# How fc's weight columns reach the partitions: matrix products on TensorE, or row transfers and a block transpose on VectorE

## The chip, the cores and the metric

The kernel runs on one core of one Trainium2 chip. A core has a matrix engine (TensorE, in the profile PE, with its weight loads as PEld), a vector engine (VectorE, DVE), a scalar engine (ScalarE, ACT), GpSimd (POOL), a queue engine for transfers (SyncE, SP) and 16 DMA engines that all of them share. The metric is the device time of one execution in microseconds, as the median of several runs.

## The reference

Three layers of a "compressed interaction network" and one linear read-out, on a batch of 1024 rows (F = 39 fields, E = 64 numbers per field, H = 64 outputs per layer):

```python
def _cin_layer(Xk, X0, W, b):
    Wr = W.reshape(O, Hk, Fdim)
    return jnp.einsum('bhe,bfe,ohf->boe', Xk, X0, Wr) + b[None, :, None]
X0 = sparse_embedding
Xk = X0
outs = []
for W, b in ((W0, b0), (W1, b1), (W2, b2)):
    Xk = _cin_layer(Xk, X0, W, b)
    outs.append(Xk.sum(axis=-1))
cin_output = jnp.concatenate(outs, axis=-1)
return cin_output @ fc_w.T + fc_b
```

`fc_w` is one row of 192 numbers: 64 for each layer. Since only sums over E of the layers' outputs reach the result, a part of the read-out can be drawn into the weights: layer 2 and fc's third part become a small matrix V2, and V2 with W1 and fc's second part becomes weights that are multiplied with products of two fields.

## The kernel before

**The main loop.** The batch is cut into 32 blocks of 32 rows, each 2048 columns (row times E). Of every block the products of pairs of fields are formed by VectorE, 128 pairs at a time (line 219 for six full tiles of pairs, line 221 for a rest that two blocks share), and multiplied by TensorE with prepared weights `wa` into four PSUM banks (line 561; the rest by lines 581 and 592). Four product buffers let VectorE run ahead. ScalarE and VectorE finish a block (lines 609, 611, 622). The operands `r`, `u` and `v` of the products are rows of x, gathered by GpSimd with indirect transfers (line 174) whose row numbers stand in the tile `lists`. The order of the work on each engine is written out by hand; nothing is reordered.

**The head.** Before the first product of line 561 the weights must be made, and the first rows gathered. In the order of TensorE:

- `spin` (line 279) multiplies constants into a bank that nobody reads: a dummy, which only keeps the engine occupied. Lines 287, 341, 411, 509, 513 and 669 call it.
- fc's columns. `fc_w` is loaded as one row on one partition (line 250, SP's queue). GpSimd writes its second and third part with each number doubled (`double`, line 320, four copies), and TensorE turns rows into columns, as products with a single 1 (`turn`, line 323): two for the doubled columns behind the first dummy, three more (columns for the finishing of blocks and for the read-out) at lines 510 to 512. They land in the bank `small`.
- V2: `fc2`, which VectorE makes from the first doubled column and a mask (line 357), times `w2s` (line 403, eight instructions), then two block transposes of VectorE (line 422), then two small products that spread the result (line 435), and VectorE writes `v2` (lines 448 and 455; the last one uses the second doubled column).
- The transposes of W0 (line 415), and T: `v2` times `w1s` (line 484, eight instructions), whose four results VectorE transposes (line 493). From there come the pair weights (lines 500 to 528), the turned weights (lines 545 to 547) and the first real product.

**VectorE in the head** runs, in its order: memsets (lines 245 to 249), a chain of small operations on 128 numbers for the index lists (lines 309 and 343 to 363, the lists are ready with lines 362 and 363), in the midst of it `fc2` (line 357), then `unit` and `twice` (lines 371 to 375), more of the index work (lines 380 to 384), and the transposes of line 422.

**The transfers in the head.** ScalarE's queue issues `w2s`, the first half of x's first block (`xh`), `w0s`, `w1s` and the second half, in this order (lines 252 to 260). GpSimd writes a row of ones to DRAM (line 366) and then gathers; its first gather (line 389) needs the first `xh` and the lists.

```python
def turn(dst, row):
    nc.tensor.matmul(dst, row, one, start=True, stop=True)
```

Of the kernel before, what the change touches and what calls it, by code (L numbers as in the profile page):

```python
# [54 lines left out]
F32 = mybir.dt.float32  # L55
I32 = mybir.dt.int32
AF = mybir.ActivationFunctionType
ALU = mybir.AluOpType
AX = mybir.AxisListType

B, F, E, H = 1024, 39, 64, 64
# [14 lines left out]
MM = 512  # L76
# [10 lines left out]
NY = 3  # L87
# [60 lines left out]
def cin_kernel(ctx: ExitStack, tc: tile.TileContext, x, w0t, b0, w1, b1, w2, b2, fc_w, fc_b, out):  # L148
    nc = tc.nc
# [3 lines left out]
    const = ctx.enter_context(tc.tile_pool(name="const", bufs=1))  # L153
# [9 lines left out]
    def bank(name):  # L163
        return psum.tile([128, MM], F32, name=name, tag="po")
# [23 lines left out]
    wa = const.tile([128, NCHUNK, 3 * H], F32, name="wa")  # L188
    columns = const.tile([128, 3], F32, name="columns")
    v2 = const.tile([128, 128], F32, name="v2")  # L190
    v2v = v2.rearrange("p (low s b) -> p low s b", s=2, b=32)
    twice = const.tile([128, H, 2], F32, name="twice")
    b2s = const.tile([H, 1], F32, name="b2s")
    b1s = const.tile([128, 1], F32, name="b1s")
    b0s = const.tile([128, 1], F32, name="b0s")
    fc0s = columns[:, 1:2]
    fcb = const.tile([NY * 32, 1], F32, name="fcb")
# [8 lines left out]
    ones = const.tile([16, 2, 128], F32, name="ones")  # L206
# [18 lines left out]
    with prep as prep:  # L225
# [3 lines left out]
        flat = prep.tile([128, 4, NA, 32], F32, name="flat")  # L229
        fcrow = prep.tile([1, 3 * H], F32, name="fcrow")  # L230
        fcrow2 = prep.tile([1, 2, H, 2], F32, name="fcrow2")
        fc2 = prep.tile([128, H], F32, name="fc2")
# [10 lines left out]


        nc.vector.memset(ones, 1.0)
        nc.vector.memset(fc2, 0.0)
        nc.vector.memset(v2, 0.0)
        nc.vector.memset(warm, 0.0)
        nc.vector.memset(wfin[0:H], 1.0)
        nc.sync.dma_start(fcrow, fc_w)  # L250
        def load_half(k):
# [21 lines left out]
        pw = [bank("pw") for _ in range(2)]  # L273
        small = bank("small")


        def spin(n=1, cols=MM // 2):
            for _ in range(n):
                nc.tensor.matmul(  # L279
                    idle[:, 0:cols],  # L280
                    nc.const_aps.tensor(1.0, (128, 128), F32),
                    nc.const_aps.tensor(1.0, (128, cols), F32),
                    start=True,
                    stop=True,
                )
# [13 lines left out]
        def step(x, at, by, out=None):  # L299

            out = new() if out is None else out
            nc.vector.tensor_scalar(out, x, at, by, ALU.is_ge, ALU.mult)
            return out
# [8 lines left out]
        for i in range(NT):  # L312
            at = OFFSET[i] - 3 * K + (0 if i < NT - 1 else -F)
            for k, by in enumerate((STEP[i], BASE[i], at)):
                nc.gpsimd.memset(shifts[:, k, i : i + 1], float(by))
        one = ones[0:1, 0, 0:1]

        def double(dst, src):
            for s in range(2):
                nc.gpsimd.tensor_copy(dst[:, :, s], src)  # L320

        def turn(dst, row):
            nc.tensor.matmul(dst, row, one, start=True, stop=True)

        def turn_row(h, at, row, k):
            turn(small[h : h + H, at : at + 1], row[:, k * H : k * H + H])

        def turn_twice(at, row, k):
            turn(small[:, at : at + 1], row[:, k].rearrange("p h s -> p (h s)"))

        double(fcrow2[:, 1], fcrow[:, 2 * H : 3 * H])
        double(fcrow2[:, 0], fcrow[:, H : 2 * H])
        for k, series in enumerate((U_STEPS, V_STEPS)):
# [4 lines left out]
        nc.gpsimd.memset(bothv[0:H, :, F], 0.0)  # L338
        for at, k in ((0, 1), (6, 0)):
            turn_twice(at, fcrow2, k)  # L340
        spin(1, 3 * MM // 4)

        nc.vector.tensor_copy(row, place)
        step(row, F, 1.0, j)
        step(row, K + ONLY, 1.0, late)
# [10 lines left out]
        )  # L356
        nc.vector.tensor_scalar(fc2[:, 0::32], mask, small[:, 0:1], None, ALU.mult)
        step(wide[:, 1], F, -float(F), wide[:, 2])
# [95 lines left out]

        nc.vector.tensor_scalar(v2v[:, 0, :, F - 32], mask, small[:, 6:7], None, ALU.mult)

# [39 lines left out]
        for k, a in groups:  # L496
# [4 lines left out]
            if k > 1:  # L501
# [6 lines left out]
                )  # L508
        spin(1, MM)
        for h in (0, H):  # L510
            turn_row(h, 1, fcrow, 0)
        turn_row(0, 2, fcrow, 2)
        spin(1, MM)
        first = [prods.tile([128, BLK], F32, name="p", tag="p") for _ in range(3)]
# [125 lines left out]
    def last_weights(pk):  # L640
        for low, at, n in ((1, 0, 32), (0, 32, F - 32)):
            nc.tensor.matmul(
                pk[at : at + n, 0:1], v2v[:, low, 0, 0:n], b1s, start=True, stop=True
            )
        fc1 = v2v[:, 0, 0, F - 32 : FT - 32]
        total = pk[0 : NY * 32, 1:2]
        nc.tensor.matmul(total, b1s.to_broadcast([128, NY * 32]), fc1, start=True, stop=False)
        nc.tensor.matmul(
            total, b2s.to_broadcast([H, NY * 32]), columns[0:H, 2:3], start=False, stop=True
        )  # L650
        nc.scalar.copy(wfin[H : H + F], pk[0:F, 0:1])
        nc.scalar.activation(kfin, total, AF.Identity, bias=fcb, scale=float(E))
# [10 lines left out]
    for k, (n, c) in enumerate(steps[:3]):  # L663
# [11 lines left out]
        else:  # L675
            product(n, c, halves[0], p[n, c])
    nc.scalar.copy(columns[0:H, 1:3], small[0:H, 1:3])
    nc.scalar.copy(fc0s[H:128], small[H:128, 1:2])
    for n, c in steps[:3]:
# [128 lines left out]
```

## Time and profile before

| | |
|---|---|
| median of 3 runs | 733.39 us (732.57 to 735.92) |
| the profiled execution's own time | 733.53 us |
| its span, first to last instruction | 731.5 us |
| mean granted TensorE clock | 0.999 |
| PE busy | 726.7 us, 99% of the span |
| DVE busy | 638.2 us, 87% |
| POOL busy | 401.0 us, 55% |
| DMA | mean 270 GB/s |
| first product of line 561 begins | 17.40 us after the span's start |

All times inside the profile are counted from the first instruction; 2.0 us of the device time lie around the span. [...] an interval of "busy" TensorE can also be slow TensorE: the time from one product to the next has to be read beside it. [...]

### The profile page before, as it was taken

To read this page: it belongs to the slowest core of one execution; us is meant where nothing else is said; L and a number is where in the kernel's file an instruction comes from. 1 tells how busy PE (TensorE), PEld (TensorE's weight loads), DVE (VectorE), ACT (ScalarE), POOL (GpSimd) and SP (SyncE) were. 2 spreads that over 40 slices of the span, in tenths; PEclk is the share of its full clock that TensorE was granted. 3 is DMA by queue.
4 is the path that set the end of the run, shared out by engine and by line. 5 is a ranking of instruction groups with operands and counts; after the bars stand their busy time and mean duration, and the time that the engine had idled before them with its cause. 6 is when DMAs were issued, how large, how long until landed. Compare 5 with 4: busy or idle time off the path is not lost.

```text
span 731.5 us, 6359 instructions
## 1 busy us (share of the span) xinstructions
PE 726.7 (99%) x2379; PEld 315.3 (43%) x2379; DVE 638.2 (87%) x521; ACT 167.0 (23%) x240; POOL 401.0 (55%) x254
## 2 busy tenths in 40 slices
PE   9999999999999999999999999999999999999998
PEld 4444444444444444444444444444444444444443
DVE  6989699988889988889988889888898988889885
ACT  3332121222212222121222212222121221212222
POOL 6779869636555445754537555455654547545300
PEclk9999999999999999999999999999999999999999
DMA  8986796989575787757679575886767777566700
GB/s 273 378 322 251 304 367 247 382 324 366 219 283 222 284 339 279 277 226 280 273 288 326 230 280 222 310 345 233 280 244 278 299 287 280 197 267 234 288 0 1
DMA packets 65983, 197.24 MB, mean 270 GB/s; under 512 B 40110, under 2 KB 40179, under 8 KB 45984
## 3 DMA queue, kind: packets, MB, share of 16 engines
q0 software_dynamic: 28784, 185.56, 64.9%
q1 hardware_dynamic: 35468, 9.29, 5.5%
q10 hardware_dynamic: 1700, 1.99, 0.9%
q8 instruction: 18, 0.29, 0.2%
q14 instruction: 13, 0.11, 0.0%
HBM read 196.76 MB, written 10.60 MB: 283 GB/s over the span
## 4 chain that ended last, share of the span: by engine, by line
PE 87%; DVE 5%; issue 3%; DMA 2%; POOL 2%; ACT 0%; DVEq 0%; POOLq 0%
PE po L561 80%; PE po L581 4%; DVE p L219 3%; PE po L592 2%; POOL r L174 2%; DVE g L611 1%; DMA r<-xd,lists 1%; DMA b0s<-in_b 1%; PE idle L279 1%; DVE sums L622 1%; DVE pairs L528 0%; PE pv L403 0%; PE pt L484 0%; PE pw L415 0%; PE pv L484 0%
## 5 line engine op out<-in xcount | busy, mean ns | idle before, releaser
L561 PE MATMUL po<-p,wa 128*128 128x512 f32 x1536 | 665.2, 593 | 0.6 <-DVE p L219 0.5
L219 DVE TENSOR_TENSOR p<-r 128x2048 f32<-128x2048 f32 (+2 forms) x198 | 433.8, 2223 | 72.8 <-PE po L561 63.8
L174 POOL DMA_INDIRECT r<-xd,lists x156 | 316.3, 2028 | 264.4 <-issue 255.0
L561 PEld LDWEIGHTS po<-p,wa 128*128 128x128 f32 x1536 | 289.7, 190 | 371.9 <-issue 353.7
L609 ACT ACTIVATE z<-po,columns 64x512 f32<-64x512 f32 x128 | 87.4, 683 | 374.2 <-PE po L592 216.0
L611 DVE SCALAR_TENSOR_TENSOR g<-po,b0s,z 64x512 f32<-64x512 f32 x128 | 95.9, 749 | 9.3 <-ACT z L609 5.3
L604 ACT COPY g<-r 39x1024 f32<-39x1024 f32 x64 | 66.7, 1043 | 161.5 <-DVE sums L622 129.7
L622 DVE TENSOR_REDUCE sums<-g 103x16 f32<-103x1024 f32 x62 | 75.6, 1219 | 2.1
L174 POOL DMA_INDIRECT u<-xd,lists x16 | 40.1, 2509 | 7.1 <-issue 4.6
L581 PE MATMUL po<-p,wa 32*64 32x512 f32 x512 | 31.6, 600 | 0.0
L174 POOL DMA_INDIRECT v<-xd,lists x16 | 26.5, 1659 | 4.9 <-issue 4.9
L221 DVE TENSOR_TENSOR p<-u,v 128x1024 f32<-128x1024 f32 x16 | 19.5, 1216 | 0.0
L581 PEld LDWEIGHTS po<-p,wa 32*64 32x64 f32 x512 | 9.4, 131 | 20.1 <-issue 20.1
L592 PE MATMUL po<-u,wa 32*64 32x512 f32 x256 | 17.0, 587 | 0.0
L174 POOL DMA_INDIRECT r<-xh,lists x8 | 8.0, 1002 | 4.7 <-DVE tmp L384 2.6
L592 PEld LDWEIGHTS po<-u,wa 32*64 32x64 f32 x256 | 5.8, 132 | 8.1 <-issue 8.0
L279 PE MATMUL idle<-const-float32-1.0 128*128 128x512 f32 (+2 forms) x12 | 7.7, 732 | 0.8 <-PEq L795 0.8
L528 DVE TENSOR_TENSOR pairs<-both 128x2 f32<-128x2 f32 (+27 forms) x59 | 6.1, 172 | 0.3
L546 ACT COPY wa<-tr 128x128 f32<-128x128 f32 x8 | 2.1, 266 | 15.3 <-PE tr L545 15.3
L279 PEld LDWEIGHTS idle<-const-float32-1.0 128*128 128x128 f32 x12 | 2.5, 253 | 1.9 <-issue 1.7
L168 POOL DMA_DIRECT2D xd<-in_x x3 | 3.2, 1056 | 0.0
L461 ACT COPY both<-pw 64x468 f32<-64x468 f32 (+2 forms) x4 | 1.9, 472 | 4.4 <-issue 4.3
(97 smaller groups left out, 55.2 us busy)
## 6 DMA issues: line engine op xcount, KB each, us to landing
xd<-in_x SPq DMA_DIRECT2D x28, 312.0 KB
r<-xd,lists POOLq DMA_INDIRECT x156, 9.1
xd<-in_x POOLq DMA_DIRECT2D x3, 312.0 KB
w2s<-in_w ACTq DMA_DIRECT2D x1, 624.0 KB
w1s<-in_w ACTq DMA_DIRECT2D x1, 624.0 KB
w0s<-in_w0t ACTq DMA_DIRECT2D x1, 380.2 KB
xh<-in_x ACTq DMA_DIRECT2D x2, 156.0 KB
xd<-xh SPq DMA_DIRECT2D x2, 156.0 KB
```

The costliest lines, as they stand in the source:

```text
L174: nc.gpsimd.indirect_dma_start(dst, None, table, bass.IndirectOffsetOnAxis(ap=lists[:, k : k + 1], axis=0))
L219: nc.vector.tensor_tensor(p[:, cols], r[:, i, cols], r[:, k, cols], ALU.mult)
L221: nc.vector.tensor_tensor(p[:, 0:SUB], ut[n // 2 % 2], vt[n // 2 % 2], ALU.mult)
L279: nc.tensor.matmul(idle[:, 0:cols], nc.const_aps.tensor(1.0, (128, 128), F32), nc.const_aps.tensor(1.0, (128, cols), F32), start=True, sto ...
L528: nc.vector.tensor_tensor(out, diagonal(a, b, sa, sb), diagonal(b, a, sb, sa), ALU.add)
L561: nc.tensor.matmul(po[n][m], wa[:, c, side : side + 2 * H], p[:, bass.ts(m, MM)], start=n % 2 == 0 and c == 0, stop=n % 2 == 1 and c == NP ...
L581: nc.tensor.matmul(dst[half * H : half * H + H], wa[rows, NPAIR, at : at + H], p[rows, bass.ts(side, MM)], start=t >= 2, stop=t < 2 and ha ...
L592: nc.tensor.matmul(dst[half : half + H], wa[rows, NPAIR + 1, H : 2 * H], ut[n // 2 % 2][rows, bass.ts(side, MM)], start=False, stop=t < 2,)
L604: nc.scalar.copy(gt[H : H + F], rt[n % 2][0:F, 0, bass.ts(m, SUB)])
L609: nc.scalar.activation(z[one], po[n][m][other], AF.Identity, bias=fc0s[other])
L611: return lambda: nc.vector.scalar_tensor_tensor(g[n][m // 2][0:H, at], po[n][m][one], b0s[one], z[one], ALU.add, ALU.mult)
L622: nc.vector.tensor_reduce(sums[:, b_at : b_at + SB], g[n][m // 2].rearrange("p (b e) -> p b e", e=E), AX.X, ALU.add,)
```

## The change

fc's columns no longer go through GpSimd and TensorE. Three small row transfers on SP's queue bring pieces of `fc_w` to four partitions (0, 32, 64 and 96): one brings fc's second and third part, 16 numbers to a partition, for the doubled columns, and two bring its first and third part, 32 numbers to a partition. VectorE clears both tiles first, copies the 16 numbers twice each into the row tile, and transposes it in blocks of 32 by 32 (one instruction, 128x128); each column of interest is then the first column of a block in `columns`, in SBUF. The copy and the transpose stand in VectorE's order behind `row <- place` and ahead of the index chain.

On TensorE the five `turn` products (ten instructions) are gone, the second dummy has 512 columns in place of 384, and the two dummies behind T stand together. GpSimd's four copies, the bank `small` and ScalarE's two copies out of it are gone. Everything else is as before; its lines have other numbers.

```diff
-    columns = const.tile([128, 3], F32, name="columns")
+    columns = const.tile([128, 4, 32], F32, name="columns")
-    fc0s = columns[:, 1:2]
+    fc1t, fc2t, fc0s, fc2s = (columns[:, k, 0:1] for k in range(4))
...
-        fcrow = prep.tile([1, 3 * H], F32, name="fcrow")
-        fcrow2 = prep.tile([1, 2, H, 2], F32, name="fcrow2")
+        fcq = prep.tile([128, 2, 16], F32, name="fcq")
+        fcrow = prep.tile([128, 4, 32], F32, name="fcrow")
...
+        nc.vector.memset(fcq, 0.0)
+        nc.vector.memset(fcrow, 0.0)
         nc.vector.memset(ones, 1.0)
...
-        nc.sync.dma_start(fcrow, fc_w)
+        nc.sync.dma_start(
+            fcq[0::32], fc_w.rearrange("o (k g j) -> (o g) k j", k=3, j=16)[:, 1:3]
+        )
+        halves_of = fc_w.rearrange("o (k g j) -> (o g) k j", k=3, j=32)
+        for h in (0, H):
+            nc.sync.dma_start(fcrow[h : h + H : 32, 2:4], halves_of[:, 0:3:2])
...
-        double(fcrow2[:, 1], fcrow[:, 2 * H : 3 * H])
-        double(fcrow2[:, 0], fcrow[:, H : 2 * H])
...
-        for at, k in ((0, 1), (6, 0)):
-            turn_twice(at, fcrow2, k)
-        spin(1, 3 * MM // 4)
+        spin(1, MM)
 
         nc.vector.tensor_copy(row, place)
+        nc.vector.tensor_copy(
+            fcrow[:, 0:2].rearrange("p k (j s) -> p k j s", s=2),
+            fcq.unsqueeze(3).to_broadcast([128, 2, 16, 2]),
+        )
+        nc.vector.transpose(
+            columns.rearrange("p k j -> p (k j)"), fcrow.rearrange("p k j -> p (k j)")
+        )
         step(row, F, 1.0, j)
...
-        nc.vector.tensor_scalar(fc2[:, 0::32], mask, small[:, 0:1], None, ALU.mult)
+        nc.vector.tensor_scalar(fc2[:, 0::32], mask, fc2t, None, ALU.mult)
...
-        nc.vector.tensor_scalar(v2v[:, 0, :, F - 32], mask, small[:, 6:7], None, ALU.mult)
+        nc.vector.tensor_scalar(v2v[:, 0, :, F - 32], mask, fc1t, None, ALU.mult)
...
-        spin(1, MM)
-        for h in (0, H):
-            turn_row(h, 1, fcrow, 0)
-        turn_row(0, 2, fcrow, 2)
-        spin(1, MM)
+        spin(2, MM)
...
-            total, b2s.to_broadcast([H, NY * 32]), columns[0:H, 2:3], start=False, stop=True
+            total, b2s.to_broadcast([H, NY * 32]), fc2s[0:H], start=False, stop=True
...
-    nc.scalar.copy(columns[0:H, 1:3], small[0:H, 1:3])
-    nc.scalar.copy(fc0s[H:128], small[H:128, 1:2])
```

More of the change, by code (lines that the diff above doesn't have):

```diff
@@ L273, in cin_kernel @@
         pw = [bank("pw") for _ in range(2)]
-        small = bank("small")
         def spin(n=1, cols=MM // 2):
@@ L315, in cin_kernel @@
                 nc.gpsimd.memset(shifts[:, k, i : i + 1], float(by))
[L316 to L329, printed above, removed]
-        double(fcrow2[:, 1], fcrow[:, 2 * H : 3 * H])
-        double(fcrow2[:, 0], fcrow[:, H : 2 * H])
         for k, series in enumerate((U_STEPS, V_STEPS)):
```

## The prediction, made before the changed kernel had run

> **What bounds the kernel.** First the page: engines' busy time, and the group of the main loop.
>
> ```profile
> PE 726.7 (99%) x2379; PEld 315.3 (43%) x2379; DVE 638.2 (87%) x521; ACT 167.0 (23%) x240; POOL 401.0 (55%) x254
> ...
> L561 PE MATMUL po<-p,wa 128*128 128x512 f32 x1536 | 665.2, 593 | 0.6 <-DVE p L219 0.5
> ```
>
> TensorE sets the end: once line 561 has begun (17.40 in TensorE's timeline) it waits 0.6 us in all. The span is a head of 17.4, the loop, and a tail of about 5 behind it. The change touches the head alone, so its worth is how far it moves 17.40, as long as the loop is fed. So, second, the chain that ended last, at its beginning (start, duration, what):
>
> ```profile
> 0.77 2.05 PE idle L279 x2
> ...
> 2.83 1.01 PE small L323 x4
> 3.83 1.58 PE idle L279 x2
> 5.41 2.33 PE pv L403 x8
> 7.74 1.15 PE idle L279 x2
> 8.89 0.55 PE pv L435 x4
> 9.44 1.56 PE pw L415 x7
> 11.00 2.15 PE pt L484 x4
> 13.15 1.17 PE pv L484 x4
> ```
>
> The light products of line 323 are on it. The last two rows are the same work, four instructions of 320 columns each, at 0.54 and 0.29 us apiece: up to about 12.9 TensorE runs at half rate, though the page prints its clock as full. Third, VectorE's timeline (start, duration, what, idle before and its releaser):
>
> ```profile
> 2.98 0.21 DVE L354 TENSOR_SCALAR wide<-wide,tmp 128x1 f32<-128x1 f32 x1
> 3.87 0.23 DVE L357 TENSOR_SCALAR fc<-mask,small 128x2 f32<-128x2 f32 x1 [0.69 <-PE small L323]
> ...
> 4.87 0.17 DVE L362 CAST lists<-fields_of 128x5 int32<-128x5 f32 x1
> ...
> 7.79 0.52 DVE L422 STREAM_TRANSPOSE blocks<-pv 128x320 f32<-128x320 f32 x1 [0.55 <-PE pv L403]
> ...
> 23.06 2.45 DVE L219 TENSOR_TENSOR p<-r 128x1024 f32<-128x1024 f32 x2 [0.32 <-DMA r<-xh,lists]
> ```
>
> VectorE waits 0.69 for fc's column, but by then much of the index chain is behind it. At 23.06 it waits for gathered rows. Last, how a small transfer fares among the loads: GpSimd's timeline, then the DMA view from 4.5 to 7.4 (packets, MB, share) and from 7.4 to 8.8.
>
> ```profile
> 3.74 0.76 POOL L366 DMA_DIRECT2D xd<-ones  x1
> 7.11 1.05 POOL L174 DMA_INDIRECT r<-xh,lists  x1 [2.60 <-DVE tmp L384]
> ```
>
> ```profile
> q10 hardware_dynamic: 507, 0.79, 93.2%
> ```
>
> ```profile
> q10 hardware_dynamic: 418, 0.36, 87.9%
> q0 software_dynamic: 16, 0.01, 2.1%
> ```
>
> The ones (16 KB, queue q0) were issued by 4.50, yet none of their packets ran before 7.4: they stood behind ScalarE's loads (q10) for some 2 to 3 us. The row of fc before (0.8 KB) was issued at 0.73 and had landed by the trace's semaphore records at 1.99; its packet ran at 1.66, ahead of the loads' first at 1.76.
>
> [...] half rate until 3.5 us after line 435's light products ended at 9.4. [...]
>
> **The change, part by part.**
>
> *The transfers.* They must wait for two memsets, which VectorE starts at 0.85. Those cost 0.1 and 0.17 (rows of `fc2` and `v2`), so the first goes at about 1.00 and the others at 1.37 and 1.74, at 0.35 to 0.4 of SP each (line 250 took 0.35; behind them SP has nothing until 10.46). At 1.26 each, as before, the last would land at 3.00: the lower bound. But they reach the DMA engines at 1.9 to 2.7 (0.93 after issue, as fc's row did), and `w2s` is there from 1.76 until 3.7 to 4.8; then the first `xh`, whose wait on GpSimd ends at 6.27; then `w0s`. Behind `w2s` and some of `xh` the last lands at 4.0 to 5.4; behind `w0s` too at up to 7.5, the upper bound. I take 4.6.
>
> *VectorE.* A copy (0.22, row of line 374; it is done before the last landing) and a transpose of 128 columns: between 0.15, VectorE's smallest, and 0.52, line 422; I take 0.3. `columns` is ready at T = 4.6 + 0.35 = 4.95 (bounds 3.35 and 7.85). What is queued behind this wait: the whole index chain, `fc2`, `unit`, `twice`. Formerly they ran at 1.52 to 3.19 less 0.3 of waiting (1.36), and then from 3.87 to 6.48 (2.61). `fc2` is ready at T + 1.36 + 0.2 = T + 1.6, the lists at T + 2.5, and line 384 ends at T + 3.9.
>
> *TensorE.* The first two dummies, at half rate 0.85 an instruction, end at about 4.3 (0.77, 1.76, then 0.85 each). V2 then starts at T + 1.6 = 6.55, where it started at 5.34 (`w2s` allows 4.86). The two transposes of line 422 follow line 384 or V2, whichever is later, and line 435 starts at T + 3.9 + 2 x 0.52 + 0.1 = T + 5.05, where it was 8.82. So the head moves by T - 3.77: +1.2. What was removed, 1.0 of light products at 2.83 and some 0.3 at 15.1, gives nothing back: at 2.83 the wait for T replaces it, and at 15.1 line 545 waits for VectorE's line 528 (ends at 16.35), which covers it. If T were below 3.77 the gain ends at 4.86, at -0.5.
>
> *The clock.* Light products end about 10.6, not 9.4. If full rate comes 3.5 us after, it moves along, and nothing is added. [...] all eight instructions of T run slow: 4 x (0.54 - 0.29) = 1.0 more. Half: +0.5. The sum is +1.7 on 17.40.
>
> *Gathers.* GpSimd starts its first gather at 7.11, after the wait for `xh` at 6.27. The lists at 7.45, with 0.3 to 0.8 to start, give 7.75 to 8.25: about +0.9 for all landings. GpSimd's four copies (0.83) saved are worth nothing, it then waits anyway. Rows +0.9 and TensorE +1.7 keep the loop fed; and the 0.6 that TensorE waited near 101, for products that had waited for rows, may shrink by half: -0.3.
>
> *The rest* costs nothing. ScalarE's two copies out of `small` (0.31) stood where ScalarE idles. `fc2` and `v2` read a scalar in SBUF, not PSUM. The read-out's product changes its operand's place only.
>
> *Sum:* 1.2 + 0.5 - 0.3 = +1.4 on the profiled 733.53, so 734.9. That execution was 0.14 above the median of the runs; I leave 734.9.
>
> **Rivals.**
>
> 1. *The small transfers slip in* (0.20). For it: [...] that `w2s` is only starting at 1.9. Against it: the ones at 4.5. The last lands at 3.0 to 3.4, T is 3.35 to 3.75, V2 starts at 4.95 to 5.3[...]. This ends below before. But the gain is capped: rows land as before (23.06), VectorE is busy from there to the product (0,4), which ends at 31.70, and TensorE takes it at 32.35. TensorE can start 0.65 earlier and then waits. 732.8 to 733.6. It decides from T below 3.77.
> 2. *They stand behind `xh` and `w0s`* (0.22). For it: the sixteen packets of the ones ran at 7.44 to 9.61 in the trace, beside the landings of `w1s` (7.45 to 9.94). Landing at 5.6 to 7.5, T at 5.95 to 7.85, head +2.2 to +4.1, clock +0.5, give-back 0.3 to 0.6, rows at most equally late: +2.2 to +4.3, 735.7 to 737.8. This one passes 0.5%, slower, from T = 7.3.
> 3. *A gather falls into a stretch where it is slow* (0.08). One `u` gather took 14.6 us at 52.19, while VectorE formed six products without pause. Shifted lists could put a gather of the first blocks there, and TensorE would run out of products: +3 to +6, 736.5 to 739.5. Against it: four product buffers, and the loop starts later too.
>
> **How the numbers follow.** The likeliest case (0.50): landing at 4.0 to 5.4, T 4.35 to 5.75, head +0.6 to +2.0, clock 0 to 1.0, give-back 0 to 0.6, so +0.4 to +2.8: 733.9 to 736.3, its own range, 734.9 inside. The rivals have 0.20, 0.22 and 0.08. Eight in ten: from the lower end of rival 1, 732.8, up to 737.5, which leaves out the end of rival 2 and most of rival 3. Half a per cent, 3.7 us, is about what a measurement of this kernel can tell from no change. Faster by it: no case reaches, 0.02. Slower by it, over 737.1: a third of rival 2, most of rival 3 and a little for what I don't see, 0.16. Within: 0.82.
>
> **What would show it.** Right: three transfers on SP from 1.0; VectorE idle ahead of the 128x128 transpose until about 4.6; the first gather at 7.7 or later; V2 at about 6.5 and line 435's counterpart at about 10; TensorE idle behind its second dummy for some 2 us; the first product of the main loop at 18.5 to 20. Wrong: the transpose before 3.7 (rival 1), T's first half at 0.29 an instruction (an earlier full clock), the gathers no later while the head is, or TensorE waiting in the loop for products (rival 3).

## The result and the profile after

| | before | after |
|---|---|---|
| median | 733.73 us (732.57 to 736.11, 13 runs) | 738.31 us (737.28 to 742.23, 13 runs) |
| ratio | | 1.0066, 95% interval 1.005 to 1.0082 |
| the profiled execution's own time | 733.53 us | 739.03 us |
| its span | 731.5 us | 737.3 us |
| first product of the main loop | 17.40 us | 20.32 us |

The changed kernel is slower by 0.66%, 4.8 us on a median of 733.7. (The ratio is estimated from all runs; the medians themselves lie 4.6 us apart.) The forecast was 734.9 and its range ended at 737.5: the sign of the shift was right, its size was not. The profiled execution lost 5.8 us of span, and the profile names two places for most of it.

**First place: the head.** TensorE's timeline of the changed kernel (start, duration, what, idle before and its releaser):

```profile
0.77 3.75 PE L285 MATMUL idle<-const-float32-1.0 128*128 128x512 f32 x4 [0.77 <-PEq L783]
8.58 2.40 PE L397 MATMUL pv<-w2s,fc 128*64 128x320 f32 x8 [4.06 <-DVE fc L351]
...
12.07 0.62 PE L429 MATMUL pv<-blocks,twice 64*128 64x20 f32 x4
...
20.32 1.12 PE L551 MATMUL po<-p,wa 128*128 128x512 f32 x2
```

V2 (line 397, formerly 403) waits 4.06 us for `fc2`, and starts at 8.58 in place of 5.34. Line 429 (formerly 435) is 3.25 later, the first product 2.92 later. What `fc2` waited for stands in VectorE's timeline:

```profile
4.99 0.20 DVE L331 COPY fcrow<-fcq 128x64 f32<-128x64 f32 x1 [3.32 <-DMA fcq<-in_fc_w]
6.93 0.31 DVE L335 STREAM_TRANSPOSE columns<-fcrow 128x128 f32<-128x128 f32 x1 [1.75 <-DMA fcrow<-in_fc_w]
...
8.31 0.22 DVE L351 TENSOR_SCALAR fc<-mask,columns 128x2 f32<-128x2 f32 x1
...
9.29 0.17 DVE L356 CAST lists<-fields_of 128x5 int32<-128x5 f32 x1
```

VectorE stands still for 5.07 us in two waits, and the whole index chain is behind them: the lists are ready at 9.5, 4.4 later than before, and GpSimd's first gather goes at 9.75 (7.11 before). The transfers themselves, SyncE's timeline of the changed kernel and then the DMA view from 3.0 to 7.0 us (packets, MB, share of the engines' time):

```profile
0.92 0.74 SPq L252 DMA_DIRECT2D fcq<-in_fc_w  x1
1.73 1.07 SPq L257 DMA_DIRECT2D fcrow<-in_fc_w  x2
```

```profile
q10 hardware_dynamic: 899, 1.15, 94.8%
q1 hardware_dynamic: 24, 0.00, 0.4%
```

All three were issued by 2.80. By the semaphore records of the trace they had landed at 4.89, 5.50 and 6.81. Their 24 packets (q1) trickled through between 899 packets of ScalarE's loads (q10).

**Second place: the main loop.** The page's group of line 551, then the waits of TensorE from 24 us to the end, first before and then after (waited for: total, times, longest):

```profile
L551 PE MATMUL po<-p,wa 128*128 128x512 f32 x1536 | 665.4, 593 | 2.5 <-DVE p L219 2.4
```

```profile
PE po L561 <- DVE p L219: 0.5, 1, 0.5
```

```profile
PE po L551 <- DVE p L219: 2.4, 3, 1.2
```

TensorE now runs out of products three times (at 45.9, 60.8 and 106.4), for 1.9 us more than before. With 2.92 of the head that makes 4.8 of the 5.8 us; of the rest 0.4 lies in the tail (the small products behind the loop began 5.2 us ahead of the span's end before, 5.6 after); where the other 0.6 lies was not found. The chain that ended last runs from the small transfers to two gathers:

```profile
1.73 0.53 SPq L257
2.30 4.50 DMA fcrow<-in_fc_w
6.93 0.31 DVE columns L335
...
9.75 1.08 POOL r L174
...
24.57 4.54 POOL u L174
29.11 0.30 issue
29.42 2.96 POOL v L174
```

Two gathers stand on it with 4.54 and 2.96 us. In GpSimd's timeline of the kernel before they are

```profile
22.91 0.94 POOL L174 DMA_INDIRECT u<-xd,lists  x1 [2.53 <-DVE p L219]
24.15 0.95 POOL L174 DMA_INDIRECT v<-xd,lists  x1 [0.30 <-issue]
```

and VectorE's timeline shows what differs. Before:

```profile
20.38 2.35 DVE L219 TENSOR_TENSOR p<-r 128x1024 f32<-128x1024 f32 x2
```

VectorE had formed two half products by 22.75, waited 0.32 us for rows, and went on at 23.06 (the row shown with the prediction); the u gather began at 22.91, inside that wait. After:

```profile
23.55 4.61 DVE L219 TENSOR_TENSOR p<-r 128x1024 f32<-128x1024 f32 x4
28.09 1.06 DVE L518 TENSOR_TENSOR pairs<-both 128x28 f32<-128x28 f32 x11
...
43.57 2.29 DVE L219 TENSOR_TENSOR p<-r 128x2048 f32<-128x2048 f32 x1 [4.44 <-DMA r<-xd,lists]
```

Four products without a pause; the u gather, begun at 24.57, ends 0.95 us after they do (28.16). Everything on GpSimd behind it is late, so VectorE waits 4.44 us for the second block's rows at 43.57, and its lead over TensorE is spent.

From experiment 5 on two theories stood against each other. **A:** the head costs 2.9, because a wait for the small transfers has taken the place of the light products; and the loop's new waits come from the u and v gathers, which met VectorE's products instead of a pause. **B:** the loop waits because the head, lists and rows are late as such, or because VectorE has become too busy. The expectations of experiments 1 to 4 are older and use the letters for theories of their own; in 1 and 4 their A (late lists make rows late, and the loop starves) is a part of what is called B here.

### The profile page after: what moved, and what is told of

The parts are those of the page before. It is cut to its first block, busy times and chain, and to the rows that moved or that the text cites. A ratio compares the mean times of both kernels' runs of the same rounds, so it can differ in the third digit from the quotient of the medians.

```text
span 737.3 us, 6342 instructions
## 1 busy us (share of the span) xinstructions
PE 726.0 (98%) x2369; PEld 314.3 (43%) x2369; DVE 638.0 (87%) x525; ACT 166.8 (23%) x238; POOL 405.4 (55%) x250
## 4 chain that ended last, share of the span: by engine, by line
PE 85%; DVE 5%; DMA 4%; POOL 3%; issue 3%; ACT 0%; SPq 0%; DVEq 0%; POOLq 0%
PE po L551 80%; PE po L571 4%; DVE p L219 2%; POOL r L174 2%; PE po L582 2%; DVE g L601 1%; DMA r<-xd,lists 1%; DMA b0s<-in_b 1%; DMA xd<-in_x 1%; POOL u L174 1%; DMA fcrow<-in_fc_w 1%; DVE sums L612 1%; POOL v L174 0%; DVE sums L623 0%; ACT z L599 0%
## 5 line engine op out<-in xcount | busy, mean ns | idle before, releaser
L174 POOL DMA_INDIRECT u<-xd,lists x16 | 43.7, 2734 | 5.6 <-issue 4.6
L174 POOL DMA_INDIRECT v<-xd,lists x16 | 28.5, 1783 | 4.9 <-issue 4.9
L285 PE MATMUL idle<-const-float32-1.0 128*128 128x512 f32 (+1 forms) x12 | 7.5, 745 | 0.8 <-PEq L783 0.8
L397 PE MATMUL pv<-w2s,fc 128*64 128x320 f32 x8 | 2.4, 753 | 4.1 <-DVE fc L351 4.1
```

Of the source, the lines that this page charges most:

```text
L174: nc.gpsimd.indirect_dma_start(dst, None, table, bass.IndirectOffsetOnAxis(ap=lists[:, k : k + 1], axis=0))
L285: nc.tensor.matmul(idle[:, 0:cols], nc.const_aps.tensor(1.0, (128, 128), F32), nc.const_aps.tensor(1.0, (128, cols), F32), start=True, sto ...
```

## The experiments

Every experiment was timed beside the kernel before on the same chip; these yardsticks had medians of 733.94 (the first four), 734.91 (the next four) and 735.25 us (the last three), so ratios are compared, not microseconds.

**1. Lists first.** In the changed kernel the copy, the transpose and `fc2` move behind the index chain:

```diff
-        nc.vector.tensor_copy(fcrow[:, 0:2]..., fcq...)
-        nc.vector.transpose(columns..., fcrow...)
         step(row, F, 1.0, j)
...
         nc.vector.tensor_scalar(most, r, 23.0, 2.0, ALU.min, ALU.mult)
+        nc.vector.tensor_copy(fcrow[:, 0:2]..., fcq...)
+        nc.vector.transpose(columns..., fcrow...)
+        nc.vector.tensor_scalar(fc2[:, 0::32], mask, fc2t, None, ALU.mult)
```

> The changed kernel with the copy, the block transpose and fc2 moved behind the index chain on VectorE; the transfers stay. Theory A (two effects: fc2 late makes the head late, the lists late make the rows late and the loop starve): the first gather is back at 7.1, fc2 still waits for the last small transfer (about 6.8) and V2 starts at about 7.6, the loop's first product at about 19.5, and TensorE's waits in the loop fall from 2.8 us to 0.6 or less. Total 735.3 to 736.3, some 2 to 3 below the changed kernel. Rival B (the loop's waits come from the later head as such, not from the rows): head about the same 19.5, but waits near 2.8 remain, 737.5 to 738.5.

Measured: 738.48 us (737.06 to 739.16), ratio 1.0058 (1.004 to 1.0076). The first gather went at 7.80, nearly as early as before, and the first product at 19.67; still the waits in the loop were 3.1 us. GpSimd's and VectorE's timelines:

```profile
22.90 5.57 POOL L174 DMA_INDIRECT u<-xd,lists  x1 [2.27 <-DMA xd<-in_x]
```

```profile
22.90 4.62 DVE L219 TENSOR_TENSOR p<-r 128x1024 f32<-128x1024 f32 x4
```

Early lists alone bring nothing, so the A of this expectation failed where it put the loop's waits down to late lists. Its B, the later head as such, met the number; this run alone can't exclude it (experiment 9 bears on it). The trace shows that the rows are there, so VectorE has no pause left, and that the u gather starts with its products and ends 0.95 us behind them.

**2. The small transfers first.** They go on ScalarE's queue, ahead of the loads:

```diff
-        nc.sync.dma_start(
+        nc.scalar.dma_start(
             fcq[0::32], fc_w.rearrange("o (k g j) -> (o g) k j", k=3, j=16)[:, 1:3]
         )
...
-            nc.sync.dma_start(fcrow[h : h + H : 32, 2:4], halves_of[:, 0:3:2])
+            nc.scalar.dma_start(fcrow[h : h + H : 32, 2:4], halves_of[:, 0:3:2])
```

> The changed kernel with the three small transfers on ScalarE's queue ahead of its five loads, so that no load is before them. Theory A (they were slow because they stood behind the loads): each lands 1.3 to 1.8 after its issue begins, the block transpose starts at 3.5 to 4.2 in place of 6.93; w2s then lands at 6.5 to 7 and bounds V2 instead, so the time is no proof. Rival D (their shape is slow: four or two partitions, 64 or 128 bytes): they take 3 to 4.5 here too, transpose at 6 or later.

Measured: 736.66 us (735.97 to 737.26), ratio 1.0038 (1.0021 to 1.0056). ScalarE's, VectorE's and TensorE's timelines:

```profile
0.93 1.19 ACTq L252 DMA_DIRECT2D fcq<-in_fc_w  x1
2.16 1.09 ACTq L257 DMA_DIRECT2D fcrow<-in_fc_w  x2
```

```profile
4.49 0.31 DVE L335 STREAM_TRANSPOSE columns<-fcrow 128x128 f32<-128x128 f32 x1 [1.05 <-DMA fcrow<-in_fc_w]
```

```profile
7.61 1.89 PE L397 MATMUL pv<-w2s,fc 128*64 128x320 f32 x8 [3.09 <-DMA w2s<-in_w]
```

The last one began to be issued at 2.74, 0.44 later than on SyncE's queue, and VectorE waited for it until 4.49 in place of 6.93: standing among the loads costs 2.4 us or more. But the three issues hold ScalarE for 2.3 us, `w2s` comes later, and V2 waits for that instead, until 7.61. The first product comes at 18.84 (+1.4). Here VectorE did wait for rows (0.65 us, until 25.08), the u gather took 0.94 in that wait, and TensorE waited 0.8 in the loop. This expectation's A fits, though the transpose came a little after its 4.2; D, which needed 6 or later, doesn't.

**3. No transfers at all.** `columns` is filled with a constant; fc's numbers and the copy and transpose are left out.

```diff
+        nc.vector.memset(columns, 0.05)
-        nc.sync.dma_start(fcq[0::32], ...)
-            nc.sync.dma_start(fcrow[h : h + H : 32, 2:4], halves_of[:, 0:3:2])
-        nc.vector.tensor_copy(fcrow[:, 0:2]..., fcq...)
-        nc.vector.transpose(columns..., fcrow...)
```

> The changed kernel without its three transfers, copy and transpose: columns is filled with a constant, so fc's numbers are left out. It has no light products before V2 and no wait for fc. Theory A: V2 starts at about 4.9, when w2s has landed; the head gains, but rows land as before and the loop waits for them: 732.5 to 733.5, at most 0.3% below before. If the light products were what kept TensorE slow (rival C): T's first four instructions at 0.29 and not 0.53, [...] first product of the loop at 15.5 to 16.3; the total then 731.5 to 733, and the loop waits for rows near 23 to 32. If they were not: T's first four at 0.53, first product at 16.5 to 17.

Measured: 733.21 us (731.53 to 734.92), ratio 0.9991 (0.9982 to 1.0). TensorE's and VectorE's timelines:

```profile
14.41 1.12 PE L535 MATMUL po<-p,wa 128*128 128x512 f32 x2
```

```profile
20.05 1.23 DVE L219 TENSOR_TENSOR p<-r 128x1024 f32<-128x1024 f32 x1 [0.99 <-DMA r<-xh,lists]
22.36 2.48 DVE L219 TENSOR_TENSOR p<-r 128x1024 f32<-128x1024 f32 x2 [1.09 <-DMA r<-xh,lists]
```

This is the most that the change could bring if the columns came for nothing. The head is 3.0 us shorter, and 0.1% comes of it: VectorE waits for rows twice, and TensorE for its products. The cap that the first rival named is there: the rows, not TensorE, limit an earlier start. The first product came before either forecast (15.5 at the earliest). T's second four instructions followed the first four after 1.24 us, 0.31 apiece and not 0.53, which points to rival C; but the rate turns full at very different times in the traces of heads that do the same work (see "The clock" below), so one trace neither shows nor excludes C.

**4. Later rows in the kernel before.** GpSimd clears a tile that nobody reads four times ahead of its first gather:

```diff
+        pause = prep.tile([128, 1024], F32, name="pause")
+        for _ in range(4):
+            nc.gpsimd.memset(pause, 0.0)
```

> The kernel before with four memsets of 128x1024 on GpSimd ahead of its first gather (an estimate from the row of the 128x128 iota, 0.22: about 1.1 each, first gather at 9.5 to 10 in place of 7.11). V2 is not late. Theory A: the head stays within 0.5 of 17.4, and the loop waits for rows: 2 to 3.5 us in all, total 735.5 to 737. Rival B: rows that are 2.6 late cost nothing or up to 0.7, total 733.5 to 734.5.

Measured: 735.6 us (734.55 to 738.38), ratio 1.0033 (1.0014 to 1.0051). It isn't a clean test: beside GpSimd's memsets `fc2` took 1.64 us on VectorE in place of 0.23, so the head grew too (first product 18.27). The first gather went at 8.69, 1.58 late. VectorE then waited longer for rows (0.69 and 1.05), the u gather took 0.94 in such a wait, and TensorE's waits on VectorE from 24 us on were 0.7. The total lies at the lower end of A's range, but not for A's reason: A had the head unchanged and waits of 2 to 3.5 us. Late rows kept the pause open here; they did not bring the collision about.

**5. A break in the four products** of the changed kernel:

```diff
-    for n, c in steps[:3]:
+    for k, (n, c) in enumerate(steps[:3]):
+        if k == 1:
+            weight_rows(steps[3][1])
         product(n, c, halves[1], p[n, c])
     n, c = steps[3]
-    weight_rows(c)
```

> The changed kernel with one edit: the seven small weight rows that VectorE forms behind its third second-half product stand between the first and the second of these products, so that its run of four products without a pause (23.55 to 42.0) has a break of some 0.9 us behind the first one. Theory A (the loop's new waits come from the u gather of GpSimd, which runs beside VectorE's products without a pause and takes 4.5 us in place of 0.94): the u gather ends soon after the break begins, in 1 to 2.5 us, TensorE's waits in the loop fall from 2.8 to about 1, and the time is 736 to 736.8. Theory B (the loop waits because everything in the head is late, and VectorE has too much to do): the waits stay, and the time is 738 to 738.8. The head is the same for both, first product of the main loop at 20.3.

Measured: 740.28 us (737.9 to 743.49), ratio 1.0065 (1.0049 to 1.008): as slow as the changed kernel, as B said, where A expected half of the loss back. GpSimd's and VectorE's timelines:

```profile
24.46 0.94 POOL L174 DMA_INDIRECT u<-xd,lists  x1 [1.99 <-DMA xd<-in_x]
25.70 2.18 POOL L174 DMA_INDIRECT v<-xd,lists  x1 [0.30 <-issue]
28.18 5.23 POOL L174 DMA_INDIRECT r<-xd,lists  x1 [0.30 <-issue]
```

```profile
27.83 4.62 DVE L219 TENSOR_TENSOR p<-r 128x1024 f32<-128x1024 f32 x4
```

The u gather got in, as A said, and the next gather but one was caught by the four products now standing behind the break; it ended 0.96 us after them. In this execution (738.42, near the shortest) TensorE waited 1.0 in the loop, not 2.4, while the first product was later than in the changed kernel (21.29), since the last transpose of line 487 waited 2.3 us, for what the profile doesn't clearly show. I moved the collision; I did not take it away. How the typical execution of this version spends its 740 us is not shown by the trace of a short one.

**6. The collision forced on the kernel before,** by one memset of 128x1024 on GpSimd (0.97 us) just ahead of its u gather:

```diff
+        pause = prep.tile([128, 1024], F32, name="pause")
+        nc.gpsimd.memset(pause, 0.0)
         roll_small(0)
```

> The kernel before with one edit: GpSimd clears a tile of 128x1024 that nobody reads (about 1 us) just ahead of its u gather at 22.9, so that the gather comes to VectorE's products after VectorE's wait for rows (22.75 to 23.06) is over. The head is untouched, first product at 17.4. Theory A: the u gather, 0.94 before, takes 2.5 us or more because the products leave it no pause, the u and v rows are late by 2.5 to 4.5, and TensorE waits 1 to 2 us more in the loop: 734.8 to 735.9. Theory B: the gather takes 0.94, one us later, and the time is 733.6 to 734.2.

Measured: 734.56 us (733.62 to 738.1), ratio 0.9998 (0.9983 to 1.0013). In the median nothing happened, and A's number failed. The profiled execution (737.63) is not typical: it lies 3.1 us above the median. It had the collision,

```profile
21.93 4.53 POOL L174 DMA_INDIRECT u<-xd,lists  x1 [2.15 <-DMA xd<-in_x]
```

with four products of VectorE at 20.87 to 25.49 and waits of 3.1 us in the loop. So such an execution does cost about 3 us, but it is not this edit that brings it about: as the row shows, the gather waited another 2.15 us for `xd` after the memset, which moved nothing. How often each case comes, the trace of one execution can't say.

**7. The transpose split, and behind the lists.** `fc2` needs only the first transfer. The two blocks of the later ones are transposed some 7 us later (their columns are read from about 42 us on):

```diff
         nc.vector.tensor_scalar(lists[:, NT : 2 * NT], fields_of, ...)
+        nc.vector.tensor_copy(fcrow[:, 0:2]..., fcq...)
+        nc.vector.transpose(columns[:, 0:2]..., fcrow[:, 0:2]...)
+        nc.vector.tensor_scalar(fc2[:, 0::32], mask, fc2t, None, ALU.mult)
...
         nc.vector.tensor_scalar(v2v[:, 0, :, F - 32], mask, fc1t, None, ALU.mult)
+        nc.vector.transpose(columns[:, 2:4]..., fcrow[:, 2:4]...)
```

> The changed kernel with two edits: VectorE's copy and transpose stand behind the index lists, and the transpose takes only the two blocks that come from the first transfer (landed at 4.89); the two blocks of the other transfers are transposed some 7 us later, since their columns are read first at about 42. Theory A (what the change costs is the wait of VectorE and all behind it for the last landing, 6.81, which nobody needs that early): fc2 is ready at about 5.5, V2 starts at 5.5 to 5.7, the first gather at about 7.3, the first product of the main loop at 17.4 to 17.8, the u gather again meets a pause, and the time is 733.2 to 734.6, as before. Theory B (the transfers load the DMA queues, and the missing light products or the dummies' order change TensorE's rate): first product at 18.5 or later, 735.5 to 737.

Measured: 733.72 us (732.26 to 738.43), ratio 0.9984 (0.9966 to 1.0002). VectorE's timeline, TensorE's, and GpSimd's:

```profile
4.85 0.20 DVE L350 COPY fcrow<-fcq 128x64 f32<-128x64 f32 x1
5.08 0.24 DVE L354 STREAM_TRANSPOSE columns<-fcrow 128x64 f32<-128x64 f32 x1
5.36 0.23 DVE L358 TENSOR_SCALAR fc<-mask,columns 128x2 f32<-128x2 f32 x1
```

```profile
15.63 1.12 PE L556 MATMUL po<-p,wa 128*128 128x512 f32 x2
```

```profile
22.24 0.94 POOL L174 DMA_INDIRECT u<-xd,lists  x1 [1.33 <-DVE p L219]
```

No wait of VectorE for the transfers is left, the first product of this trace comes even earlier than in the kernel before, and the u gather meets a pause. All of the loss is undone. The three transfers are those of the changed kernel, so in themselves they cost nothing: what cost was that VectorE waited for them. The same kernel was measured again, for a narrower interval:

> The same kernel as in the run of the split transpose behind the lists (ratio 0.9984, interval 0.9966 to 1.0002), in five rounds for a narrower interval. If what costs in the change is only the wait for the two later transfers and the place ahead of the index chain, this version is at least as fast as the kernel before: 0.997 to 0.9995. If the earlier number was chance, it is 1.000 or above.

Measured: 734.21 us (733.15 to 738.52), ratio 0.9996 (0.998 to 1.0013). It is as fast as the kernel before, and not shown to be faster, which fits the cap seen in experiment 3. TensorE's timeline of this repeat:

```profile
18.01 1.12 PE L556 MATMUL po<-p,wa 128*128 128x512 f32 x2 [0.61 <-issue]
```

The same kernel has its first product at 15.63 in one trace and at 18.01 in the other, with device times of 732.53 and 733.23 us. So the start of the loop in a single trace scatters by more than 2 us, and a head can't be priced from it alone.

**8. The split alone,** with copy and transpose where the change put them:

```diff
         nc.vector.transpose(
-            columns.rearrange("p k j -> p (k j)"), fcrow.rearrange("p k j -> p (k j)")
+            columns[:, 0:2]..., fcrow[:, 0:2]...
         )
...
+        nc.vector.transpose(columns[:, 2:4]..., fcrow[:, 2:4]...)
```

> The changed kernel with one edit: the first transpose takes only the two blocks of the first transfer (landed at 4.89), at the place that the change gave it; the other two blocks are transposed some 7 us later. Theory A (the wait for the last landing, 6.81, is what costs): the transpose runs at about 5.1 and ends at 5.4, 1.85 earlier than in the changed kernel, fc2 at 6.5, first gather at about 8, first product of the main loop at about 18.7, and by my rule, head = T - 3.77, it is 1.5 later than before; with the u gather in a pause or not, 735 to 736.8. Theory B (the order on VectorE is what costs): first product at 19.5 or later, 737 to 738.5.

Measured: 735.43 us (734.06 to 739.18), ratio 1.0 (0.9985 to 1.0016). The transpose ran at 5.13, fc2 at 6.44, the first product came at 18.72, as A said; the time is better than A's 1.5 us of loss (the interval reaches to +1.2 us), and no run shows why. The profiled execution (738.26, again far above its median) had the collision, a u gather of 4.27 us and 3.5 us of waits. With 7 this shows which part of the change costs: the wait for the last landing, which nothing needed before 42 us.

**9. The changed kernel without the first u and v gathers.** Two plain transfers of the same size on SyncE's queue fill u and v with other numbers:

```diff
-        roll_small(0)
         roll(1)
...
             fill_ones(1, nc.sync, ones1)
+            flatx = x.rearrange("b f e -> (b f e)")
+            for k, dst in enumerate((ut, vt)):
+                nc.sync.dma_start(dst[0], flatx[k * 128 * SUB : (k + 1) * 128 * SUB]...)
```

> The changed kernel with one edit: GpSimd's first u and v gathers (4.54 and 2.96 us there) are left out, and two plain transfers of the same size on SP's queue, issued at about 27, fill u and v instead, with other numbers of x, so the rest tile of the first two blocks holds wrong products. The head is the same, first product at 20.3. Theory A (the two gathers that stand behind VectorE's products are what makes the loop wait): the gathers of the second block begin some 8 us earlier, its rows are there before VectorE asks (VectorE's wait for rows at about 41 falls from some 5 us to under 1), TensorE's waits in the loop fall from 2.8 to below 1, and what is left over before is the head alone, 2.9: the ratio to the kernel before is 1.003 to 1.0045 (about 736.5). Theory B (the loop waits because the head is late in itself, or for another thing): the ratio stays at 1.006 or above.

Measured: 737.4 us (734.5 to 739.71), ratio 1.0028 (1.0015 to 1.004). TensorE's waits from 24 us to the end are now those of the read-out alone:

```profile
PE py L753 <- DVE sums L622: 0.4, 1, 0.4
PE py L742 <- ACT wfin L640: 0.2, 1, 0.2
```

**10. The same edit on the kernel before:**

> The kernel before with the same edit: no first u and v gathers, plain transfers of the same size on SP's queue at about 24 in their place, with other numbers of x. It is the yardstick for the changed kernel without these gathers. Theory A: in the kernel before the u gather meets a pause of VectorE in most executions, so leaving it out is worth little: ratio 0.998 to 1.000, and the executions near 737 that the kernel before also shows become rare. Theory B: the gathers have no part in the loop's waits: 1.000. If the ratio falls to 0.996 or below, the gathers cost the kernel before as much as the changed one, and theory A explains no difference between the two.

Measured: 734.88 us (732.89 to 737.47), ratio 0.9997 (0.998 to 1.0014). Executions above 736 did not become rare (3 of 12; 13 of 43 of the kernel before), so the u gather alone is not their cause. The pair speaks for A: without these two gathers the changed kernel's loss falls from 0.66% (0.5 to 0.82) to 0.28% (0.15 to 0.40), that is by 2.8 us, and the kernel before gains nothing. What is left, 2.1 us (1.1 to 2.9), A puts down to the head. The trace of experiment 9, the longest of its twenty executions, shows the head by itself: VectorE waited for the last small transfer until 8.42, the first product came at 23.43, 6.0 us later than before, TensorE never waited for products from 24 us on, and the span was 6.4 us longer. So a late head as such does not make the loop wait, and in this execution it was paid for almost in full. Experiment 8, with a first product 1.3 later and no loss in the median, warns against making that a rule. One more thing stands in this trace:

```profile
26.75 5.28 POOL L174 DMA_INDIRECT r<-xd,lists  x1 [0.30 <-issue]
26.46 4.62 DVE L219 TENSOR_TENSOR p<-r 128x1024 f32<-128x1024 f32 x4
```

With u and v gone an r gather was held by the four products instead, for 5.28 us, and the loop did not wait. A held gather is not a loss in itself; by this account it costs when GpSimd's later gathers then come after VectorE needs them. The u and v gathers took 7.5 us of GpSimd's time in the changed kernel and 1.9 in the kernel before.

**The gather and the products,** in all traces that have this gather. "Run" is VectorE's row of products around the u gather, from the timelines.

| kernel | u gather began | took | VectorE at that time | end of the gather less end of the run |
|---|---|---|---|---|
| before | 22.91 | 0.94 | waits for rows, 22.75 to 23.06 | |
| experiment 2 | 24.57 | 0.94 | waits for rows, until 25.08 | |
| experiment 3 | 21.84 | 0.94 | waits for rows, until 22.36 | |
| experiment 4 | 25.21 | 0.94 | waits for rows, until 25.73 | |
| experiment 7 | 22.24 | 0.94 | waits for rows, until 22.76 | |
| experiment 5 | 24.46 | 0.94 | small operations, until 24.57 | |
| experiment 7, repeated | 22.65 | 1.07 | two products, 20.56 to 22.91 | 0.81 |
| after | 24.57 | 4.54 | four products, 23.55 to 28.16 | 0.95 |
| experiment 1 | 22.90 | 5.57 | four products, 22.90 to 27.52 | 0.95 |
| experiment 6 | 21.93 | 4.53 | four products, 20.87 to 25.49 | 0.97 |
| experiment 8 | 22.97 | 4.27 | four products, 21.66 to 26.28 | 0.96 |

A u gather that began while VectorE formed no product took 0.94 us, whatever followed. One that came during a run ended 0.8 to 1.0 us after the last product of it. In the runs of four, each product about 1.15 us, the u gather did not get in; what held it, the traces don't show.

It is no rule that only the end of a run lets a gather in. The v gather of the kernel before (24.15 to 25.10, shown above) lies across the two products of the row at 23.06: it ended 0.81 us after the first (24.29), while the second ran to 25.51. The rows of that second product landed only at 24.27, 0.02 before the first one ended. The v gathers of experiments 2, 3, 4, 7 and its repeat got in in the same way, between two products 0.00 to 0.04 us apart. In the runs of four each product begins, by the record, some 0.07 us before the one ahead of it has ended. Whether that overlap is what shuts a gather out was not tested, and one gather of the kernel before (43.52 to 45.98) did get in between two products of 128x2048 that overlap by 0.08.

## Why the prediction was wrong

**The transfers' landing (a size, too small).** I took 0.35 to 0.4 us for an issue, from a transfer of one row to one partition. To four and two partitions they took 0.74, 0.53 and 0.50, so the last went out at 2.80 and not at 2.1. I put the landing at 4.6 with an upper bound of 7.5; it was 6.81, within the bounds. In experiments 1, 5 and 9, with the same three transfers, VectorE waited for the last one until 7.12, 7.28 and 8.42 (6.93 in the changed kernel), in experiment 9 beyond my bound. T was 7.24 in place of 4.95. That is the second rival's case ("They stand behind `xh` and `w0s`"), to which I gave 0.22; the ones of GpSimd, which I had seen waiting in the same way, were the right precedent, and I still let the last transfer land 2.5 us after its issue, where it took 4.0. The 24 packets of q1 ran among those of q10 (12 of them from 3.0 to 4.5 us, beside 486; 9 to 6.0, beside 340; 3 to 7.5, beside 133), and this did not make a small transfer quick.

**The head, T − 3.77 (right).** With T = 7.24 it gives +3.5; line 429 came 3.25 later and the first product 2.92. The waits that I listed behind the transpose, from the index chain to `fc2` and the lists, were those that moved. Nor did I see the obvious remedy in it: only the first of the three transfers was needed so early, and VectorE waited for the other two because one transpose covers all four blocks.

**The clock (+0.5; the pair of traces can't price it).** T's two groups of four instructions took 2.36 and 1.53 us in TensorE's timeline, as against 2.36 and 1.36 before:

```profile
14.04 2.36 PE L478 MATMUL pt<-w1s,v 128*128 128x320 f32 x4
16.19 1.53 PE L478 MATMUL pv<-w1s,v 128*128 128x320 f32 x4
```

That is 0.2 more. The trace's first clock record, at full, begins at 16.6, where it was 13.0. My +0.5 was an estimate: half of the 1.0 us that T costs more when its second four instructions, too, take 0.54 us apiece and not 0.29. Nor did the full rate simply move along with the work, as I had put it. In experiment 10, whose TensorE work up to T is that of the kernel before and whose V2 begins within 0.02 us of it, the first half of T was

```profile
9.36 1.33 PE L483 MATMUL pt<-w1s,v 128*128 128x320 f32 x4
```

and in experiment 6, again with this work, 1.33 as well, from 10.02 (2.36 from 10.79 in the kernel before). So the light products, which all three have, do not fix the moment, and which case a single execution falls into looks like chance. Nor does the full clock on the page contradict the half rate: before 13.0 that trace has no clock record, and the view prints such time as full. And the rate does not only rise: in experiment 8 V2's eight instructions took 1.38 us from 6.71 (2.40 in the changed kernel), and T's first four behind them the 2.36 again, from 11.88; the mean granted clock of that execution was 0.995. In the pair of traces line 429 was 3.25 late and the end of T 3.4; 0.5 of it was won back before the first product, for which no run shows the reason.

**Gathers: "keep the loop fed", and −0.3 (the step that failed in kind).** The first gather was 2.64 later, not 0.9, but that was not the mistake. I compared rows with TensorE. What matters is rows against VectorE: it came to its third half product 3.1 us later (about 25.9, formerly 22.75), the rows for it landed 2.1 later (25.1, formerly 23.04). The 0.32 us of waiting at 23.06, which I had shown and taken for a loss, was the gap through which the u gather got in. With it gone the u and v gathers took 7.5 us together in place of 1.9. The loop added 1.9 in the profile, and 2.8 by experiments 9 and 10, where I had −0.3. This is what carried the result out of the range: with T = 7.24 my own sum gives 3.5 + 0.5 − 0.3, or 737.2, still inside it. The third rival described this mechanism; I gave it 0.08, because I thought of four buffers and of a later loop as cover, and did not ask which pause the gather had used before.

**Their sum.** 2.9 for the head, the clock in it, and 1.9 to 2.8 for the loop give 4.8 to 5.7; measured 4.8 by the ratio and 5.5 between the profiled executions. The range ended at 737.5 because I let the second and the third rival exclude each other. One can bring the other with it: here a head 2.9 later came with the loss of VectorE's pause (in experiment 2, 1.4 later, the pause stayed).

**What held.** TensorE sets the end. The removed light products gave nothing back in the changed kernel, and an early landing would have been capped by rows (experiment 3). ScalarE's and GpSimd's saved work shows nowhere in the time.

**What stays open.** That the held u and v gathers make the loop wait is read from the traces and from experiments 9 and 10; the two edits that aimed at it directly (5 and 6) did not change the time as A forecast. Open are also why experiment 8 costs nothing in the median with a first product 1.3 us later; what the typical execution of experiment 5 does; how often the kernel before has the collision; and what lets a gather in between two products. The traces of single executions can't tell these.

## What to carry to other kernels

Before moving small operands to transfers, ask who waits for the last of them and whether it needs that one: here one transpose over four blocks made VectorE wait 1.75 us more for two blocks that were read some 35 us later, and splitting it undid the loss as far as could be measured. A few hundred bytes issued among bulk loads landed 3.2 to 4.0 us after issue in the changed kernel, and in experiment 9 VectorE waited for them until 8.42; ahead of such a wait VectorE should have other work to do first. And a short wait of VectorE can be useful to GpSimd: before removing one, look in GpSimd's timeline for what runs inside it.

## What the runs showed of the hardware

- Indirect gathers were held off by runs of VectorE's products (4.3 to 5.6 us in place of 0.94 for the u gather), plain transfers issued by GpSimd were not. Experiment 9's timelines of GpSimd and of VectorE:

```profile
42.33 0.66 POOL L468 DMA_DIRECT2D b1s<-in_b  x1
42.89 0.63 POOL L469 DMA_DIRECT2D b2s<-in_b  x1
43.41 0.65 POOL L470 DMA_DIRECT2D fcb<-in_fc_b  x1
```

```profile
42.32 8.89 DVE L219 TENSOR_TENSOR p<-r 128x2048 f32<-128x2048 f32 x4
```

  The pair of transfers just ahead of these three took 1.16 us in experiment 4, beside a product (41.82 to 44.11), and 1.16 in experiment 1, where VectorE stood still (38.5 to 43.27).
- The issue of a small transfer is not one price: 0.35 us for one row to one partition, 0.50 to 0.74 on SyncE for two and four partitions, 1.19 for the first of them on ScalarE.
- The rate of TensorE's products rose, fell and rose again inside one head: in experiment 8 four dummies of 512 columns took 3.75 us from 0.77 and 1.89 from 15.67; between them V2's eight instructions took 1.38 (2.40 in the changed kernel) and T's first four 2.36 (1.33 in experiment 10). In two traces of one and the same kernel T's first four took 1.40 us from 10.47 (experiment 7) and 2.33 from 11.21 (its repeat).
- Beside memsets of GpSimd (128x1024, about 1.0 us each) a VectorE operation of 128x2 took 1.64 us in place of 0.23 (experiment 4, where the first memset ran from 4.53 and the operation from 3.88 to 5.52). Most other small operations in that stretch took their usual 0.2 us, so this is no price.
